# Graph layer 1 with own terms computed two blocks ahead, batch norm's mean from column sums, and variances summed by VectorE

## The chip, the cores and the metric

The kernel runs on one core of one Trainium2 chip. The metric is the device time of one execution in microseconds (us). Of the kernel before there are three runs; their median is 1605.33 us (1604.46 to 1609.47).

A core has five engines with a queue each: TensorE (PE, matmuls; PEld is its weight load), VectorE (DVE), ScalarE (ACT), GpSimd (POOL) and SyncE (SP). Each works through its queue in order. An instruction that waits for a semaphore holds up all that stand behind it on the same queue. SP issues the plain DMAs, POOL the indirect ones (gathers and scatters by a list of row numbers).

## The reference

Four graph layers over 2,708 nodes of 128 features and a sparse 2708 x 2708 adjacency matrix (about 16 entries in a row and the diagonal). Each is added to its input and normalised:

```python
x = _layernorm(x + _L0_gnn_ref(x, adj))   # (adj.T @ x) / column sums of adj
x = _layernorm(x + _L1_gnn_ref(x, adj, ...))
x = _layernorm(x + _L2_gnn_ref(x, adj, ...))
x = _layernorm(x + _L3_gnn_ref(x, adj, ...))   # attention, four heads
```

The two layers that matter here:

```python
# layer 1
s = x @ msg_w[:, :D].T
d = x @ msg_w[:, D:].T
messages = gelu(s[:, None, :] + d[None, :, :] + msg_b)
aggregated = einsum('ijd,ij->id', messages, adj)
new = concatenate([x, aggregated], -1) @ upd_w.T + upd_b
h = gelu(new) + x
out = (h - mean(h)) / sqrt(var(h) + eps) * ln_w + ln_b
# layer 2
h = A @ (x @ W) + b
mean = h.mean(axis=0)
var = ((h - mean) ** 2).mean(axis=0)
h = gamma * (h - mean) * rsqrt(var + eps) + beta
out = where(h >= 0, h, 0.2 * h)
```

## The kernel before

The nodes stand in 22 blocks of 128 (the last has 20). While layer 0's sums run, the kernel searches each adjacency row for its entries and makes lists of them (DVE: `extract`), ranks the nodes by their number of entries and sorts them, so that a block needs only as many message slots as its longest list (`CAPS`, 368 slots in all). Layer 0 ends with `layer0`, which writes each node's terms `d` to the table `d_dram`, and its pair of `d` and normalised `x` to `dx_dram`, scattered by rank (L781).

The loop of layer 1 (L974) takes the blocks one turn after another in the order `TURNS`. A turn has these parts:

- `own_row` (L818) loads the block's sorted rows `x_s` from `dx_dram`, one turn ahead.
- `messages` (L827) takes the one bank of the PSUM pool `own_ps` as tile `own`. PE transposes `x_s` into it (L832), ACT copies it out (`x_st`, L833), PE multiplies it with the weights and adds the bias (L834, L835): the own terms, which stay in the same bank. Then the block's message slots come in chunks of up to eight: POOL gathers one row for each node and slot from `d_dram` (L856), DVE adds the own terms to a chunk (L858), ACT applies the gelu (L861), and DVE multiplies each slot with the adjacency value and sums it, in two running sums in the same bank (`weigh`, L846). The last of each goes to `parts` in SBUF. The chunks rotate through five buffers (`msgs`, L812).
- `spread` (L594), called at the end of `messages`, prepares lists for layer 3. DVE multiplies (L601), PE multiplies into the bank `own` (L607), DVE copies out twice (L614, L615), for two groups in most turns.
- In the first turns, `transposed` (L906) and `extract` go through the nine blocks that layer 0 left over. `transposed` writes the adjacency matrix's transpose to `at_dram` in pieces that rotate through three buffers `at_sb`; later turns do that for the other thirteen blocks.
- `update` (L868) takes the one bank of the pool `tail_ps` as tile `tail`: PE sums and transposes `parts` (L872), ACT copies (L879), PE makes the new features (L881 to L883), ACT applies the gelu (L888), DVE adds `x_s` (L889). Then two layer norms follow. Each takes its variance by `deviation` (L294): ACT squares and sums (L301), DVE makes the root by some eight small steps (`rsqrt`). The result `x_n` (L319) is scattered to `x2_dram` by POOL (L898), transposed by PE (L899) and multiplied with layer 2's weights (L903, L904).
- From turn 11 on `layer2` (L950) gathers two blocks of rows of `at_dram` per turn, and PE adds them to layer 2's sums in six banks (L957).

The order on each queue is made by a scheduler from the order of the calls, except in the part before layer 1, where DVE's order is written by hand. So the scatter of L898 stands on POOL's queue between gathers of later blocks.

The batch norm after layer 2 first adds the bias to all 22 blocks (L1052) while PE sums their columns with a matrix of ones (L1054); it makes the mean from this (L1065), subtracts it (L1069), squares on ACT (L1070) and sums the squares with PE again (L1072). Layer 3 follows, with 400 gathers of its own.

Of the kernel before, what the change touches and what calls it, by code (L numbers as in the profile page):

```python
# [81 lines left out]
GOT = 9  # L82


@with_exitstack
def gnn_resnorm_kernel(
# [126 lines left out]
    dx_dram = tables.tile([NBLK * P, 2 * D], FP, name="dx_dram")  # L213
# [80 lines left out]
    def deviation(small, n, count, h, sums, newton=True):  # L294
# [5 lines left out]
        for j in range(count):  # L300
            nc.scalar.activation(  # L301
                junk[0:n], h[:, j, :], AF.Square, bias=sums[:, j : j + 1],
                accum_out=var[0:n, j : j + 1],
            )
# [10 lines left out]
    def normalised(small, n, count, h, sums, dst, newton=True):  # L315

        var = deviation(small, n, count, h, sums, newton)
        for j in range(count):
            nc.vector.tensor_scalar(  # L319
                dst[:, j, :], h[:, j, :], sums[:, j : j + 1], var[0:n, j : j + 1],  # L320
                ALU.add, ALU.mult,
            )
# [12 lines left out]
    with ExitStack() as layer:  # L335
# [6 lines left out]
        sums_ps = part.enter_context(tc.tile_pool(name="sums_ps", bufs=7, space=PSUM))  # L342
        hand.enter_context(tc.manual_schedule(engines={engine.DVE}))
# [26 lines left out]
        def weight(src, name):  # L370
            raw = small.tile([P, P], FP, name="raw_w")
# [107 lines left out]
        def ranking(g):  # L479
# [17 lines left out]
            key_row = work.tile([P, SPLIT, P], FP, name="key_row")  # L497
# [213 lines left out]
        nc.vector.tensor_copy(deg[0:NREM, NFULL : NFULL + 1], tails[0:NREM, 3:4])  # L711
        nc.vector.tensor_scalar(zero, deg, 0.0, None, ALU.is_equal)
# [6 lines left out]
        def layer0(b0, count, n):  # L719
# [32 lines left out]
            dx = brief.tile([P, count, 2, D], FP, name=f"dx{count}", bufs=3 if count > 1 else 2)  # L752
            for j in range(count):
                nc.vector.tensor_scalar(
                    dx[0:n, j, 1, :], h[0:n, j, :], sums[:, j : j + 1], v[:, j : j + 1],
# [5 lines left out]
            for j in range(count):  # L761
                nc.tensor.transpose(
                    pt[:, j * P : j * P + n], dx[0:n, j, 1, :], ident[0:n, 0:n]
# [4 lines left out]
            for j in range(count):  # L768
# [4 lines left out]
            nc.scalar.copy(dx[0:n, :, 0, :], pm[0:n, 0:count])  # L773
            nc.sync.dma_start(
                d_dram[b0 * P : b0 * P + w, :].rearrange("(b p) w -> p b w", p=n),
                dx[0:n, :, 0, :],
# [3 lines left out]
            for j in range(count):  # L780
                did = scatter(  # L781
                    dx_dram, rank[0:n, b0 + j : b0 + j + 1],
                    dx[0:n, j].rearrange("p t d -> p (t d)"),
# [28 lines left out]
        msgs = layer.enter_context(tc.tile_pool(name="msgs", bufs=5))  # L812
# [5 lines left out]
        def own_row(b):  # L818
            n = BLOCKS[b][1]
            x_s = mine.tile([P, 2, D], FP, name="x_s", bufs=3)  # L820
            nc.sync.dma_start(
                x_s[0:n],
                dx_dram[b * P : b * P + n, :].rearrange("p (t d) -> p t d", t=2),
# [3 lines left out]
        def messages(b, x_s, three):  # L827
            n, kk = BLOCKS[b][1], CAPS[b]
            po = own_ps.tile([P, 512], FP, name="own", tag="own")
            x_st, s_ps = mine.tile([P, P], FP, name="x_st"), po[:, P : 2 * P]  # L830
            acc = (po[:, 0:P], po[:, 3 * P : 4 * P])
            nc.tensor.transpose(po[:, 0:n], x_s[0:n, 1, :], ident[0:n, 0:n])  # L832
            nc.scalar.copy(x_st[:, 0:n], po[:, 0:n])  # L833
            nc.tensor.matmul(s_ps[0:n], lhsT=x_st[:, 0:n], rhs=ws_t, start=True, stop=False)  # L834
            nc.tensor.matmul(  # L835
                s_ps[0:n], lhsT=ones[0:1, 0:n], rhs=msgb[0:1, :], start=False, stop=True
            )
# [11 lines left out]
            nc.vector.tensor_tensor(mk, mk, s_ps[0:n], ALU.add)  # L849
            nc.scalar.activation(mk, mk, AF.Gelu)  # L850
            weigh(0, mk)
            for c0, c1 in chunks_of(kk):
                kc = c1 - c0
                msg = msgs.tile([P, 8, D], FP, name="msg")
                for k in range(kc):
# [3 lines left out]
                    mk, mk, s_ps[0:n].unsqueeze(1).to_broadcast((n, kc, D)), ALU.add  # L859
# [4 lines left out]
            for i, b3 in enumerate(three):  # L864
                spread(b3, po, 256 + 64 * i)
            return x_st, parts

        def update(b, x_s, x_st, parts):  # L868
# [16 lines left out]
            x_n = mine.tile([P, 1, D], FP, name="x_n")  # L885
# [6 lines left out]
            rstd = deviation(mine, n, 1, new[0:n], s0)  # L892
# [4 lines left out]
            normalised(mine, n, 1, new[0:n], s1, x_n[0:n])  # L897
            scatter(x2_dram, perm[0:n, b : b + 1], x_n[0:n, 0, :])  # L898
# [5 lines left out]
            nc.scalar.copy(xw[0:n, b, :], px)  # L904

        def transposed(b, rows, cleared=False):  # L906
# [10 lines left out]
            for j0 in range(0, NBLK, 4):  # L917
                count = min(4, NBLK - j0)
                pt = bank.tile([P, 4, P], FP, name="pt_a", tag="bank")
                at = small.tile([P, 4, P], FP, name="at_sb", bufs=3)  # L920
# [28 lines left out]

        def layer2(k):  # L950
# [3 lines left out]
            gather(at[0:n, :], at_dram, perm[0:n, b : b + 1])  # L954
            for ib in range(NBLK) if k == 0 else ORDER:
                i0, m = BLOCKS[ib]
                nc.tensor.matmul(  # L957
# [14 lines left out]
        ahead = own_row(0)  # L972
        left = list(range(SPLIT, NBLK))
        for i, b in enumerate(TURNS):  # L974
            if i == SPLIT - 2:
                sorted_lists(1)
            x_s, ahead = ahead, own_row(TURNS[i + 1]) if i + 1 < NBLK else None
# [6 lines left out]
            x_st, agg = messages(b, x_s, three)  # L984
            for _ in range(2 if i < 1 else 1):
                if left:
# [5 lines left out]
                    if e == NBLK - 1:  # L992
                        run(place(NBLK - 2, NBLK, lists(NBLK - 2, NBLK)))
            update(b, x_s, x_st, agg)
# [7 lines left out]
            if i >= 11:  # L1002
                for k in range(2 * (i - 11), min(i, 2 * (i - 10))):
                    layer2(k)
        layer2(NBLK - 1)
# [24 lines left out]
    with ExitStack() as layer:  # L1030
# [17 lines left out]
        ps_m = own_ps.tile([P, 512], FP, name="ps_m", tag="own")  # L1048
        ps_v = tail_ps.tile([P, 512], FP, name="ps_v", tag="tail")
        for b0, count, n in quads():  # L1050
            a = accs2[b0 // 4].rearrange("p (j d) -> p j d", d=D)[0:n, b0 % 4 : b0 % 4 + count]
            nc.vector.tensor_tensor(hb[0:n, b0 : b0 + count], a, broad(b_row, n, count), ALU.add)  # L1052
            for b in range(b0, b0 + count):
                nc.tensor.matmul(  # L1054
                    ps_m[:, 0:D], lhsT=ones[0:n, :], rhs=hb[0:n, b, :],
                    start=(b == 0), stop=(b == NBLK - 1),
# [6 lines left out]
        mean = work.tile([P, D], FP, name="bn_mean")  # L1063
# [968 lines left out]
```

## Time and profile before

| | us |
|---|---|
| median of three runs | 1605.33 |
| the profiled execution | 1957.99 |
| its span, first to last instruction | 1956.3 |
| layer 0, search and lists | 0 to about 229 |
| layer 1 and layer 2's sums | 229 to 1053 |
| batch norm and tables of layer 3 | 1053 to 1165 |
| layer 3 | 1165 to 1956 |

The profiled execution is 22% longer than the median, so a time read from it is larger than its share of an unprofiled run. In the whole span PE is busy 1248.6 us (64%), DVE 1173.2 (60%), ACT 768.6 (39%), POOL 896.4 (46%). In a line of the profile's timeline stand the start, the duration, the engine, the line of the kernel, the operation, what it writes and reads, and in brackets the idle time of the engine before it with what ended it. In a line of waits stand the waiting operation, what it waited for, the sum in us, how often, and the longest. "issue" is time in which the profile shows no wait, though a wait for several semaphores can be booked to the wrong one. POOL's busy time for an indirect DMA is that of its issue.

### The profile page before, as it was taken

To read this page: it belongs to the slowest core of one execution; us is meant where nothing else is said; L and a number is where in the kernel's file an instruction comes from. 1 tells how busy PE (TensorE), PEld (TensorE's weight loads), DVE (VectorE), ACT (ScalarE), POOL (GpSimd) and SP (SyncE) were. 2 spreads that over 40 slices of the span, in tenths; PEclk is the share of its full clock that TensorE was granted. 3 is DMA by queue.
4 is the path that set the end of the run, shared out by engine and by line. 5 is a ranking of instruction groups with operands and counts; after the bars stand their busy time and mean duration, and the time that the engine had idled before them with its cause. 6 is when DMAs were issued, how large, how long until landed. Compare 5 with 4: busy or idle time off the path is not lost. (4 is left out here: it accounts for less than half of the span.)

```text
span 1956.3 us, 23628 instructions
## 1 busy us (share of the span) xinstructions
PE 1248.6 (64%) x5771; PEld 866.9 (44%) x5771; DVE 1173.2 (60%) x4900; ACT 768.6 (39%) x3134; POOL 896.4 (46%) x996
## 2 busy tenths in 40 slices
PE   7972414443345564556585647888798888877884
PEld 7972313333234453445465313445444444444444
DVE  8999536763353533343346626677678777676773
ACT  3475424542222311111111414455455555455543
POOL 1002655555544445444430454555565556555430
PEclk9985655555555576666677755677677777677675
DMA  8541547765444624332331474766475665756530
GB/s 288 228 160 41 170 94 195 202 169 145 125 90 117 173 96 96 109 132 88 141 110 37 153 222 130 190 189 194 140 206 178 173 178 153 189 159 191 153 109 7
DMA packets 164926, 289.61 MB, mean 148 GB/s; under 512 B 46850, under 2 KB 118752, under 8 KB 157679
## 3 DMA queue, kind: packets, MB, share of 16 engines
q0 software_dynamic: 60496, 190.76, 34.4%
q1 hardware_dynamic: 96739, 92.56, 15.6%
q10 hardware_dynamic: 7544, 4.69, 0.9%
q8 instruction: 48, 0.79, 0.2%
q14 instruction: 99, 0.81, 0.1%
HBM read 242.50 MB, written 45.35 MB: 147 GB/s over the span
## 5 line engine op out<-in xcount | busy, mean ns | idle before, releaser
L245 POOL DMA_INDIRECT g<-t_dram,idx x400 | 402.2, 1005 | 310.8 <-issue 169.2
L245 POOL DMA_INDIRECT msg<-d_dram,idx x368 | 348.7, 947 | 272.1 <-issue 225.7
L1324 ACT ACTIVATE sum_junk<-g 126x128 bf16<-126x128 f32 (+3 forms) x1024 | 302.6, 298 | 142.3 <-issue 60.8
L1293 PE MATMUL z<-x,copies 32*126 32x512 f32 (+3 forms) x800 | 220.3, 917 | 60.7 <-DVE g L1490 33.9
L957 PE MATMUL acc<-x_nat,at_rows 128*128 128x128 f32 (+2 forms) x968 | 168.8, 335 | 64.5 <-issue 52.6
L931 PE MATMUL pt_a<-ident,rows 128*128 128x128 f32 (+2 forms) x475 | 119.0, 408 | 131.5 <-ACT at_sb L936 106.9
L1490 DVE TENSOR_TENSOR g<-g,z 126x1536 f32<-126x1536 f32 (+3 forms) x100 | 175.1, 1751 | 40.1 <-remote 25.4
L1324 ACT ACTIVATION_READ_ACCUMULATOR sum_junk<-g 126x1 f32 (+3 forms) x1024 | 193.5, 189 | 0.0
L957 PEld LDWEIGHTS acc<-x_nat,at_rows 128*128 128x128 f32 (+2 forms) x968 | 151.2, 240 | 78.8 <-issue 67.5
L1298 PE MATMUL z<-g,ident 126*126 126x512 f32 (+3 forms) x200 | 168.5, 937 | 0.1
L1370 PE MATMUL po_s<-wm,g 126*128 126x24 f32 (+6 forms) x800 | 124.7, 310 | 59.7 <-DVE wm L1357 53.8
L931 PEld LDWEIGHTS pt_a<-ident,rows 128*128 128x128 f32 (+2 forms) x475 | 86.4, 212 | 154.8 <-ACT at_sb L936 120.9
L1370 PEld LDWEIGHTS po_s<-wm,g 126*128 126x128 f32 (+3 forms) x800 | 120.8, 237 | 75.1 <-DVE wm L1357 63.8
L1316 DVE SCALAR_TENSOR_TENSOR g<-g,a_ps 126x1536 f32<-126x1536 f32 (+6 forms) x100 | 151.1, 1511 | 0.0
L406 PE MATMUL acc<-x_nat,rows 128*128 128x129 f32 (+3 forms) x1012 | 128.5, 288 | 25.9 <-DMA rows<-in_adj_dram 15.1
L406 PEld LDWEIGHTS acc<-x_nat,rows 128*128 128x128 f32 (+2 forms) x1012 | 122.9, 197 | 31.1 <-DMA rows<-in_adj_dram 16.1
L846 DVE SCALAR_TENSOR_TENSOR own<-msg,ls,own 128x128 f32<-128x128 f32 (+1 forms) x302 | 106.5, 353 | 37.4 <-remote 13.5
L1293 PEld LDWEIGHTS z<-x,copies 32*126 32x126 f32 (+3 forms) x800 | 65.3, 250 | 97.9 <-issue 54.2
L1308 DVE SCALAR_TENSOR_TENSOR g<-z,a 126x128 f32<-126x128 f32 (+3 forms) x400 | 92.0, 287 | 19.4 <-DMA g<-t_dram,idx 9.4
L431 DVE FIND_INDEX8 ci<-cv,rows 128x8 uint32<-128x247 f32 (+2 forms) x242 | 101.6, 420 | 0.0
L436 DVE MAX8 cv<-rows 128x8 f32<-128x247 f32 (+2 forms) x242 | 98.0, 411 | 2.2 <-POOL rows L396 2.2
L1298 PEld LDWEIGHTS z<-g,ident 126*126 126x126 f32 (+3 forms) x200 | 41.7, 261 | 122.1 <-issue 109.1
(293 smaller groups left out, 2084.0 us busy)
## 6 DMA issues: line engine op xcount, KB each, us to landing
rows<-in_adj_dram SPq DMA_DIRECT2D x34, 1354.0 KB
at_dram<-at_sb SPq DMA_DIRECT2D x105, 256.0 KB
g<-t_dram,idx POOLq DMA_INDIRECT x400
msg<-d_dram,idx POOLq DMA_INDIRECT x368
t_dram<-t_row SPq DMA_DIRECT2D x21, 256.0 KB
x_s<-dx_dram SPq DMA_DIRECT2D x21, 128.0 KB
at_dram<-at_sb SPq DMA_DIRECT2D x21, 64.0 KB
d_dram<-dx SPq DMA_DIRECT2D x5, 256.0 KB
```

Of the source, the lines that this page charges most:

```text
L245: nc.gpsimd.indirect_dma_start(out=dst, out_offset=None, in_=table[0:N, :], in_offset=bass.IndirectOffsetOnAxis(ap=index, axis=0),)
L406: nc.tensor.matmul(accs0[k][0:m, c0 : c0 + f1 - f0], lhsT=rows[0:n, j0 : j0 + m], rhs=x_nat[0:n, b, f0:f1], start=k not in started, stop=( ...
L431: nc.vector.max_index(out=ci[0:n, at], in_max=cv[0:n, at], in_values=rows[0:n, c0 : c0 + cw])
L846: nc.vector.scalar_tensor_tensor(to, m, v, last, ALU.mult, ALU.add)
L931: nc.tensor.transpose(pt[0:m, j, 0:n], rows[0:n, c0 : c0 + m], ident[0:n, 0:n])
L957: nc.tensor.matmul(accs2[ib // 4][0:m, (ib % 4) * D : (ib % 4 + 1) * D], lhsT=at[0:n, i0 : i0 + m], rhs=xw[0:n, b, :], start=(k == 0 and i ...
L1293: nc.tensor.matmul(z3[0:e, r, :] if r < 3 else z1[0:e], lhsT=copies[g][rows, j, :], rhs=own[b][1][rows, :], start=True, stop=r < 3, skip_g ...
L1298: nc.tensor.matmul(z1[0:e], lhsT=ident[0:e, 0:e], rhs=g4[0:e, 3, 0:HD], start=False, stop=True, skip_group_check=True,)
L1316: nc.vector.scalar_tensor_tensor(z, z, 0.0, a_ps[0:e].unsqueeze(1).to_broadcast((e, count, HD)), ALU.max, ALU.mult)
L1324: nc.scalar.activation(junk[0:e], g4[0:e, r, hd * D : (hd + 1) * D], AF.Identity, accum_out=sc[0:e, r, hd : hd + 1],)
L1370: nc.tensor.matmul(po[:, p0 * HEADS : (p0 + g) * HEADS], lhsT=g4s[i][0:e, r, HD : HD + D], rhs=wm[0:e, 4 * i + r, :, :], start=True, stop= ...
L1490: nc.vector.tensor_tensor(z, z, z3[0:e], ALU.add)
```

## The change

- Own terms: a new function `own_terms` computes `x_st` and the own terms for a block two turns ahead, in the bank of `tail_ps` (shared with `update`), and copies them to SBUF as `s`. `messages` reads `s`. The bank of `own_ps` is taken once, as `sums1`, and held for all turns: it keeps the running sums and, in columns that alternate from turn to turn, the spread steps. Row loads go out three turns ahead (`x_s` has four buffers).
- The scatter of a block's rows is no longer called in `update` but in `put_results`, after the `messages` of the next turn.
- `msgs` has six buffers, `at_sb` five. Two tiles of the first part move to a pool `head` that is given back before layer 1.
- The variances of `update` are made by DVE: it subtracts the mean into `centred` and squares and sums that.
- Batch norm's mean: layer 0's column sums of the adjacency matrix (`column_sums`) go as one more column into the scattered rows of `dx_dram` and are loaded in sorted order by one DMA of single elements. In `layer2` ACT spreads a block's column over a tile `weighed`, and PE multiplies it with the same right side into a free part of the sixth bank of sums, so that the columns' sum over all nodes is there with the last block. The first pass of the batch norm and its matmuls with ones go away; the bias and the mean are one row, `shift`.

```diff
-    dx_dram = tables.tile([NBLK * P, 2 * D], FP, name="dx_dram")
+    DX = 2 * D + 1
+    dx_dram = tables.tile([NBLK * P, DX], FP, name="dx_dram")
...
         for j in range(count):
+            if here:
+                centred = small.tile([P, D], FP, name="centred", bufs=1)
+                nc.vector.tensor_scalar(
+                    centred[0:n], h[:, j, :], sums[:, j : j + 1], None, ALU.add
+                )
+                nc.vector.scalar_tensor_tensor(
+                    junk[0:n], centred[0:n], 1.0, centred[0:n], ALU.mult, ALU.mult,
+                    accum_out=var[0:n, j : j + 1],
+                )
+                continue
...
+        column_sums = work.tile([P, 24], FP, name="column_sums")
+        nc.vector.tensor_copy(column_sums, deg)
...
-            nc.scalar.copy(dx[0:n, :, 0, :], pm[0:n, 0:count])
+            nc.scalar.copy(dx[0:n, :, 0:D], pm[0:n, 0:count])
+            nc.gpsimd.tensor_copy(
+                dx[0:n, :, 2 * D : DX], column_sums[0:n, b0 : b0 + count].unsqueeze(2)
+            )
...
-        msgs = layer.enter_context(tc.tile_pool(name="msgs", bufs=5))
+        msgs = layer.enter_context(tc.tile_pool(name="msgs", bufs=MSGS))
...
-        def messages(b, x_s, three):
+        def own_terms(b, x_s):
+
+            n = BLOCKS[b][1]
+            tp = tail_ps.tile([P, 512], FP, name="terms", tag="tail")
+            x_st = mine.tile([P, P], FP, name="x_st", bufs=3)
+            s = mine.tile([P, D], FP, name="s", bufs=3)
+            nc.tensor.transpose(tp[:, 0:n], x_s[0:n, 1, :], ident[0:n, 0:n])
+            nc.scalar.copy(x_st[:, 0:n], tp[:, 0:n])
+            pn = tp[0:n, P : 2 * P]
+            nc.tensor.matmul(pn, lhsT=x_st[:, 0:n], rhs=ws_t, start=True, stop=False)
+            nc.tensor.matmul(pn, lhsT=ones[0:1, 0:n], rhs=msgb[0:1, :], start=False, stop=True)
+            nc.scalar.copy(s[0:n], pn)
+            return x_s, x_st, s
+
+        def messages(b, x_s, s, three, spreads):
             n, kk = BLOCKS[b][1], CAPS[b]
-            po = own_ps.tile([P, 512], FP, name="own", tag="own")
-            x_st, s_ps = mine.tile([P, P], FP, name="x_st"), po[:, P : 2 * P]
-            acc = (po[:, 0:P], po[:, 3 * P : 4 * P])
-            nc.tensor.transpose(po[:, 0:n], x_s[0:n, 1, :], ident[0:n, 0:n])
-            nc.scalar.copy(x_st[:, 0:n], po[:, 0:n])
-            nc.tensor.matmul(s_ps[0:n], lhsT=x_st[:, 0:n], rhs=ws_t, start=True, stop=False)
-            nc.tensor.matmul(
-                s_ps[0:n], lhsT=ones[0:1, 0:n], rhs=msgb[0:1, :], start=False, stop=True
-            )
+            acc = (sums1[:, 0:P], sums1[:, 3 * P : 4 * P])
...
-                    mk, mk, s_ps[0:n].unsqueeze(1).to_broadcast((n, kc, D)), ALU.add
+                    mk, mk, s[0:n].unsqueeze(1).to_broadcast((n, kc, D)), ALU.add
...
-                spread(b3, po, 256 + 64 * i)
-            return x_st, parts
+                spread(b3, sums1, P + 128 * (spreads % 2) + 64 * i)
+            return parts
...
-            normalised(mine, n, 1, new[0:n], s1, x_n[0:n])
-            scatter(x2_dram, perm[0:n, b : b + 1], x_n[0:n, 0, :])
+            normalised(mine, n, 1, new[0:n], s1, x_n[0:n], here=True)
+            results.append((b, x_n))
...
+        def put_results():
+            while results:
+                b, x_n = results.pop(0)
+                n = BLOCKS[b][1]
+                scatter(x2_dram, perm[0:n, b : b + 1], x_n[0:n, 0, :])
...
-                at = small.tile([P, 4, P], FP, name="at_sb", bufs=3)
+                at = small.tile([P, 4, P], FP, name="at_sb", bufs=5)
...
+        column_sum = keep.tile([P, NBLK], FP, name="column_sum")
+        for b0, b1, n in ((0, NFULL, P), (NFULL, NBLK, NREM)):
+            nc.sync.dma_start(
+                column_sum[0:n, b0:b1],
+                dx_dram[b0 * P : b0 * P + (b1 - b0 - 1) * P + n, 2 * D : DX].rearrange(
+                    "(b p) o -> p (b o)", p=n
+                ),
+            )
...
+            weighed = small.tile([P, P], FP, name="weighed", bufs=1)
+            nc.scalar.activation(
+                weighed[0:n], ones[0:n], AF.Copy, scale=column_sum[0:n, b : b + 1]
+            )
             for ib in range(NBLK) if k == 0 else ORDER:
                 i0, m = BLOCKS[ib]
+                if ib == 21:
+
+                    nc.tensor.matmul(
+                        accs2[5][:, 2 * D : 3 * D], lhsT=weighed[0:n], rhs=xw[0:n, b, :],
+                        start=False, stop=False,
+                    )
...
-        ahead = own_row(0)
+        sums1 = own_ps.tile([P, 512], FP, name="sums1", tag="own")
+        rows1 = [own_row(b) for b in TURNS[:3]]
+        terms = [own_terms(b, rows1.pop(0)) for b in TURNS[:2]]
...
-            x_s, ahead = ahead, own_row(TURNS[i + 1]) if i + 1 < NBLK else None
+            x_s, x_st, s = terms.pop(0)
+            if i + 3 < NBLK:
+                rows1.append(own_row(TURNS[i + 3]))
...
-            x_st, agg = messages(b, x_s, three)
+            agg = messages(b, x_s, s, three, i)
+            put_results()
...
+            if rows1:
+                terms.append(own_terms(TURNS[i + 2], rows1.pop(0)))
             update(b, x_s, x_st, agg)
...
-        ps_m = own_ps.tile([P, 512], FP, name="ps_m", tag="own")
         ps_v = tail_ps.tile([P, 512], FP, name="ps_v", tag="tail")
+        nc.vector.scalar_tensor_tensor(
+            mean, accs2[5][:, 2 * D : 3 * D], 1.0 / N, b_row, ALU.mult, ALU.add
+        )
+        nc.vector.tensor_tensor(shift, b_row, mean, ALU.subtract)
         for b0, count, n in quads():
             a = accs2[b0 // 4].rearrange("p (j d) -> p j d", d=D)[0:n, b0 % 4 : b0 % 4 + count]
-            nc.vector.tensor_tensor(hb[0:n, b0 : b0 + count], a, broad(b_row, n, count), ALU.add)
-            for b in range(b0, b0 + count):
+            h = hb[0:n, b0 : b0 + count]
+            sq = small.tile([P, 4, D], FP, name="bn_sq")
+            nc.vector.tensor_tensor(h, a, broad(shift, n, count), ALU.add)
+            nc.scalar.activation(sq[0:n, 0:count], h, AF.Square)
+            for j in range(count):
                 nc.tensor.matmul(
-                    ps_m[:, 0:D], lhsT=ones[0:n, :], rhs=hb[0:n, b, :],
-                    start=(b == 0), stop=(b == NBLK - 1),
+                    ps_v[:, 0:D], lhsT=ones[0:n, :], rhs=sq[0:n, j, :],
+                    start=(b0 + j == 0), stop=(b0 + j == NBLK - 1),
                 )
```

## The prediction

> **What bounds the kernel now.** I read the busy shares by stage first, then GpSimd's waits in layer 1, then its order in time, then one turn of the node loop, then the batch norm. Layer 1 and the sums of layer 2 run from 229 to 1053 us of a span of 1956.3 us. No engine is full there (columns: stretch, length, then busy us and instructions of PE, weight loads, DVE, ACT, POOL; clock, DMA share, GB/s):
>
> ```profile
> 229.00:698.00 469.00, 198.81 (x811) 155.50 (x812) 230.22 (x1099) 165.87 (x341) 232.57 (x245) 0.54 0.57 151
> 698.00:987.00 289.00, 158.87 (x879) 137.18 (x879) 106.65 (x436) 37.86 (x100) 146.76 (x155) 0.68 0.32 102
> ```
>
> So waits bound it. The queue with the longest steady work is POOL: an indirect DMA starts every 1.25 us (0.95 busy, 0.30 between, from the timeline below), so the 155 of the late stretch need 194 us of its 289, and the 245 of the early one 306 of 469. POOL's waits from 698 to 987 us:
>
> ```profile
> POOL msg L245 <- issue: 56.1, 133, 15.9
> POOL x_dram L253 <- DVE own L846: 49.8, 5, 14.1
> POOL x_dram L253 <- DVE x_n L319: 35.1, 3, 17.2
> ```
>
> The scatter of a finished block's rows waits for them, and every gather behind it on the queue waits too. In time, one such place:
>
> ```profile
> 740.69 0.95 POOL L245 DMA_INDIRECT at_rows<-at_dram,perm  x1 [0.31 <-issue]
> 741.94 0.95 POOL L245 DMA_INDIRECT at_rows<-at_dram,perm  x1 [0.30 <-issue]
> 756.55 1.00 POOL L253 DMA_INDIRECT x_dram<-x_n,perm  x1 [13.67 <-DVE own L846]
> ```
>
> Why the rows are late shows in the turn after 853 us. The last sums of the messages end at 853.66; the next block's transpose needs the same PSUM bank `own` and starts at 865.80, after both spread steps went through it one after the other; its first message add starts at 872.53:
>
> ```profile
> 853.05 0.61 DVE L846 SCALAR_TENSOR_TENSOR parts<-msg,ls,own 128x128 f32<-128x128 f32 x2
> ...
> 865.58 0.17 DVE L615 CAST idx<-own 125x20 int32<-125x20 f32 x1
> ...
> 865.80 0.48 PE L832 MATMUL own<-ident,x_s 128*128 128x128 f32 x1 [3.02 <-issue]
> ...
> 870.59 0.26 ACT L833 COPY x_st<-own 128x128 f32<-128x128 f32 x1
> ...
> 872.53 0.29 DVE L849 TENSOR_TENSOR x_s<-x_s,own 128x128 f32<-128x128 f32 x1 [1.31 <-PE own L835]
> ```
>
> That is 18.9 us in which no message of the next block is used; the messages themselves then take from 872.5 to 886.6, 14 us. The batch norm starts with two passes in series:
>
> ```profile
> 1053.24 0.69 DVE L1052 TENSOR_TENSOR hb<-acc,b_row 128x512 f32<-128x512 f32 x1 [9.00 <-PE acc L957]
> ...
> 1059.80 3.48 DVE L1069 TENSOR_TENSOR hb<-hb,bn_mean 128x512 f32<-128x512 f32 x7
> ```
>
> **What the Trainium skill says.** Its page "Perfetto Trace Analysis", section "DMA Instruction — SWDGE (GPSIMD)", says that the profiled interval of a DMA from GpSimd ends when the descriptors are written. The trace agrees: a gather of 128 rows of 512 bytes takes 947 ns and one of 128 rows of 10,832 bytes 946 ns. So POOL's pace counts instructions, not bytes. The same page, "Optimization Strategy", says that bubbles that repeat can mean that no buffer is free for the next tile; the bank above is such a case. Its section "Optimizing Scalar/DVE Operations" makes a VectorE operand in PSUM dearer than one in SBUF (about 125 against 60 ns). Here the add with a PSUM operand (L849) takes 289 ns and that with SBUF alone (L877) 284, so I book nothing for `s` in SBUF. "SBUF — State Buffer", section "SBUF: two separate sides", says that a VectorE operation with two SBUF inputs, or in a two-port mode, can hold a port that GpSimd needs; no row here isolates it. It gives a rival below.
>
> **The change part by part** (sums in the profiled execution's time).
>
> Bank held, own terms two blocks ahead, scatter moved. The transpose, the copy, two matmuls and their waits leave the head of the turn, and the spread steps no longer stand between two blocks. The built order confirms it: on DVE the spread multiplies now stand between message sums or small steps, and on POOL the scatter of block b stands 7 to 11 message chunks behind the block's last gather (turns 0 to 15) against 4 to 7 before. The waits that can go are 289 - 194 = 95 us from 698 to 987 us, and one of 5.4 at 1004.7. The last two scatter waits (10.1 and 16.6 us) come after the last gather and stay. Not all of the 95 is free. A turn still costs DVE its 13 us (106.65 over the eight turns) with dependent steps between, and PE the update. With turns of 36 us now (scatters 11 to 19 of 22 lie at 697.7 and 987.1, 289.4 us for eight turns) and POOL at 24, I take two thirds: 63 us, bounds 20 and 95. With the 5: 68.
>
> Early stretch, 229 to 698. POOL waits 163 us, mostly for message buffers. DVE also searches nine adjacency blocks here (242 MAX8 and 242 FIND_INDEX8 over 22 blocks, 98.0 and 101.6 us: 9 us a block) and is busy 230 us. A sixth buffer and the freed bank help less where DVE holds the work: 15 us, bounds -10 and 60.
>
> Variance on VectorE. Two ScalarE passes of 0.40 + 0.19 us leave per block; a subtract (0.35, as L319) and a square with sum (0.29 + 0.08, as L889) come twice. That is 1.4 us more DVE per block, 32 us in all, beside gathers while POOL sets the pace; uncovered it costs up to 32. Only the last block's chain is bare: about 1 us gained. Already inside the "two thirds".
>
> Batch norm. The pass to 1059.80 goes (6.56 us); two small operations come (0.29 each): 6 us gained, bare, since all later stages wait. `weighed` (22 ScalarE passes of about 0.4, as L916) and 22 matmuls of two 0.28 passes, 12 us of PE, lie in stretches where PE is busy 55%: nothing, at most 12.
>
> Column sums. Seven copies on POOL stand among the scatters of `dx_dram`, which run back to back from 215.8: some 0.3 us each, 2 us lost (bounds 0 and 4; the nearest rows are POOL's small iotas and memsets, 0.11 to 0.3). Their load moves 2,708 elements of 4 bytes. The like of it exists, the load of `diag`, and its issue held ScalarE's queue for 13.32 us:
>
> ```profile
> 16.27 13.32 ACTq L669 DMA_DIRECT2D diag<-in_adj_dram  x1
> ```
>
> It now stands on SP ahead of the first three row loads, and the first `weighed` waits for it on ScalarE ahead of the first `x_st` copy, with the gelus behind. The first add comes some 13 us later; POOL, with six chunks of buffers (45 gathers, 56 us), goes on. I take 5 us lost, bounds 0 and 13.
>
> Five `at_sb` buffers instead of three: ScalarE waits 16.1 us in all for these stores; off the path, nothing. Rows of 1,028 bytes, `head` and the fourth `x_s`: nothing. Row loads go out two turns earlier on SP.
>
> Sum: 68 + 15 + 1 + 6 - 2 - 5 = 83 us of 1957.99 (span 1956.3). That execution is 22% longer than the median of 1605.33; I scale by 1605.33 / 1957.99 = 0.82 and get 68: 1537 us.
>
> **The rivals.** (1) The waits move from the scatter to the message buffers, since DVE's and PE's turn, not the bank, sets the pace. For it: in the early stretch POOL waits for buffers already. Against it: DVE is busy only 107 of 289 us. Then a fifth of the 95, 19, stays, with 6 - 7 = -1 from the rest, 18 x 0.82 = 15: 1590 us.
> (2) Slower: own terms and update now share the single bank `tail`. The update held it from 857.7 (L872) to 883.6 (L904), 26 us; the own terms held `own` for 6.7 (865.80 to 872.5). In series 33 us: under the turn of 36, so it doesn't decide, unless a turn of both grows past 36, say by PE's order, since terms of b+2 stand ahead of the sums of b. Each us above costs 22. At 2.5 above, 55 x 0.82 = 45: 1650 us.
> (3) The port: 55 adds of about 1.0 us and 44 subtracts of 0.35 hold GpSimd off, up to 70 us, which cancels most of 83: 1595 to 1603 us, no change at worst. Against it: gathers keep 895 to 1077 ns through everything that DVE does now.
>
> **How the numbers follow.** Forecast 0.60 (1537; its own range 1500 to 1570), rival 1 0.22, rival 2 0.11, rival 3 0.07. Changes under 0.3% (5 us) can't be told from none. Faster: 0.60 + 0.22 + 0.02 of rival 3 = 0.84; same 0.05; slower 0.11. The low end is all of the 95 and half of the early bound: (95 + 5 + 30) x 0.82 = 107, 1498, and a little more: 1492. The high end takes in rival 1: 1598.
>
> **What would show it.** POOL's scatter waits before the last gather fall from 90 to under 20 us, its waits on messages don't rise by as much, and 987 moves to about 900 us. The first batch norm add and the first square lie 1 us apart. SP shows one issue of about 13 us near 230. Wrong: large POOL waits on `msg` in the late stretch (rival 1), PE waiting on `tail` or `terms` for longer each turn (2), or gathers over 1.1 us (3).

## The result: 1.0% slower

| | us | ratio to the kernel before |
|---|---|---|
| kernel before, median of 13 runs | 1606.28 | |
| kernel after, median of 13 runs | 1622.20 (1610.94 to 1631.08) | 1.0096, 95% interval 1.0073 to 1.0118 |
| forecast | 1537 (1492 to 1598) | |

The forecast had the sign wrong. Its profile is the first thing to look at again. The kernel before takes one of two times, about 1605 us in some series of runs and about 1950 us in others (medians 1934 and 1957, on other chips than the first; why is not known), and the profile that the prediction read, 1957.99 us, is of the second kind. A second profile of the kernel before, called *base* below, has a span of 1606.3 us, and the profile of the kernel after one of 1629.4, from the longest of its 13 runs. These two are compared; their difference of 23 us is more than the 16 between the medians.

First the stretch from the first to the last message gather of layer 1, by engine (stretch, length, then busy us and instructions of PE, weight loads, DVE, ACT, POOL; clock, DMA share, GB/s). The kernel before in the prediction's profile:

```profile
229.00:1014.00 785.00, 379.15 (x1806) 310.29 (x1807) 347.95 (x1583) 208.78 (x455) 396.02 (x417) 0.60 0.47 131
```

The kernel before in base:

```profile
231.00:793.00 562.00, 319.16 (x1781) 268.07 (x1782) 335.75 (x1538) 204.80 (x447) 396.37 (x417) 0.67 0.62 180
```

The kernel after:

```profile
231.00:806.00 575.00, 324.37 (x1737) 273.89 (x1736) 326.86 (x1639) 196.95 (x400) 412.92 (x416) 0.66 0.61 177
```

POOL does the same 417 instructions in the same 396 us in both profiles of the kernel before; only its waits differ. With 0.31 us between two indirect DMAs as the normal gap, the waits beyond it sum to 261 us in the prediction's profile (157 at message gathers, 101 at the scatters of L253) and to 38 in base (13 and 22). So at 1605 us POOL is close to its own pace through the whole layer, and there were 38 us to win there, not 163 + 95. In the kernel after POOL is busy 16.6 us longer with one instruction less.

The waits of POOL in that stretch in base (who waited for whom, sum, times, longest):

```profile
POOL msg L245 <- issue: 113.9, 312, 7.2
POOL x_dram L253 <- DVE x_n L319: 17.0, 1, 17.0
```

and in the kernel after:

```profile
POOL msg L249 <- issue: 97.7, 319, 0.6
POOL x_dram L257 <- DVE x_n L333: 12.0, 2, 6.4
POOL lists_dram L257 <- DVE rs_t L271: 11.2, 1, 11.2
POOL lists_dram L257 <- DMA lists_dram<-lists,rank: 5.5, 1, 5.5
```

Under "issue" the longest wait before a message gather fell from 7.2 to 0.6 us: what is left there is the 0.3 us gap, 319 times. What was gained there (11 us) and at the scatter (9 us) came back at the scatter of the lists (17 us more). The costliest group of POOL in layer 1, from the page of base (busy us, mean ns, idle before):

```profile
L245 POOL DMA_INDIRECT msg<-d_dram,idx x368 | 349.1, 949 | 132.2 <-issue 113.9
```

and of the kernel after:

```profile
L249 POOL DMA_INDIRECT msg<-d_dram,idx x368 | 365.2, 992 | 118.4 <-issue 97.7
```

The same 368 gathers take 16.1 us longer. The timeline of the kernel after shows one of them:

```profile
620.01 0.94 POOL L249 DMA_INDIRECT msg<-d_dram,idx  x1 [0.30 <-issue]
621.20 1.22 DVE L884 TENSOR_TENSOR msg<-msg,s 128x1024 f32<-128x1024 f32 x1 [9.83 <-issue]
621.25 1.99 POOL L249 DMA_INDIRECT msg<-d_dram,idx  x1 [0.30 <-issue]
623.55 0.94 POOL L249 DMA_INDIRECT msg<-d_dram,idx  x1 [0.30 <-issue]
```

The message add runs from 621.20 to 622.42; the gather that starts just after it ends at 623.24, 0.82 us after the add. The same meeting in base, where the own terms lie in PSUM, leaves the gather alone:

```profile
245.27 1.09 DVE L858 TENSOR_TENSOR msg<-msg,own 128x896 f32<-128x896 f32 x1 [3.37 <-DMA msg<-d_dram,idx]
245.36 0.94 POOL L245 DMA_INDIRECT msg<-d_dram,idx  x1 [0.30 <-issue]
```

Worked out over the whole timeline: of the 37 indirect DMAs of the kernel after that had a message add running 0.12 us after their own start, 33 end 0.78 to 0.86 us after the end of that add; in base 3 of 43 do, by chance, and their lengthening sums to nothing. An add that begins when a gather is well under way doesn't lengthen that one.

The trace shows a second thing, at the PSUM bank `tail`, which the update of a block and the own terms of a later one now share. Seven instructions around one update (parts are the finished sums of a block's messages):

```profile
712.63 0.34 DVE L872 SCALAR_TENSOR_TENSOR parts<-msg,ls,sums 128x128 f32<-128x128 f32 x1
...
722.05 0.71 PE L898 MATMUL tail<-ident,parts 128*128 128x128 f32 x4 [0.35 <-ACT s L858]
...
744.40 0.27 ACT L930 COPY x_nat<-tail 128x128 f32<-128x128 f32 x1 [0.58 <-PE tail L929]
...
744.72 0.33 PE L853 MATMUL terms<-ident,x_s 128*128 128x128 f32 x1
...
746.34 0.27 ACT L858 COPY s<-terms 128x128 f32<-128x128 f32 x1 [0.35 <-PE terms L857]
...
746.64 0.29 DVE L875 TENSOR_TENSOR x_s<-x_s,s 128x128 f32<-128x128 f32 x1 [3.56 <-ACT s L858]
...
746.88 0.61 PE L898 MATMUL tail<-ident,parts 128*128 128x128 f32 x4
```

The sums of a block are ready at 712.97, but its update starts at 746.88: first comes the update of the block before (722.05 to 744.67), then the own terms of a later block (744.72 to 746.61). On average a block's sums wait 26.1 us for their update, in base 2.6. An update holds the bank for 22.3 us and own terms for 2.9, and from the first update at 304 us to the last at 849 the bank is held 98.5% of the time, without a gap over 1 us; in base, by updates alone, 88%. Nor are the own terms early: in 15 of the 22 blocks the first add that reads `s` starts within 0.1 us of the end of its copy. VectorE's first use of the own terms in base and in the kernel after (busy us, mean ns, idle before):

```profile
L849 DVE TENSOR_TENSOR x_s<-x_s,own 128x128 f32<-128x128 f32 x21 | 6.0, 287 | 21.4 <-PE own L835 21.3
L875 DVE TENSOR_TENSOR x_s<-x_s,s 128x128 f32<-128x128 f32 x21 | 6.1, 290 | 48.2 <-ACT s L858 48.2
```

The batch norm starts 22 us later than in base, though the last message gather starts only 13 us later. The last block's sums are even just 3 us late (815.9 against 813.1), but its update starts 20 us after them, in base 2. So two things can have cost time, longer gathers and the shared bank, and the experiments have to tell them apart.

### The profile page after: what moved, and what is told of

It is laid out like the page before. It is cut to its first block, busy times and chain, and to the rows that moved or that the text cites. A ratio compares the mean times of both kernels' runs of the same rounds, so it can differ in the third digit from the quotient of the medians.

```text
span 1629.4 us, 23721 instructions
## 1 busy us (share of the span) xinstructions
PE 1175.2 (72%) x5771; PEld 828.0 (51%) x5771; DVE 1159.0 (71%) x5027; ACT 757.8 (47%) x3090; POOL 910.2 (56%) x1003
## 5 line engine op out<-in xcount | busy, mean ns | idle before, releaser
L249 POOL DMA_INDIRECT msg<-d_dram,idx x368 | 365.2, 992 | 118.4 <-issue 97.7
L1351 PE MATMUL z<-x,copies 32*126 32x512 f32 (+3 forms) x800 | 208.5, 865 | 26.6 <-DVE g L1548 25.2
L1010 PE MATMUL acc<-x_nat,at_rows 128*128 128x128 f32 (+2 forms) x968 | 156.6, 324 | 49.1 <-DMA at_rows<-at_dram,perm 48.8
L965 PE MATMUL pt_a<-ident,rows 128*128 128x128 f32 (+2 forms) x475 | 100.7, 375 | 114.7 <-ACT at_sb L970 103.8
L1010 PEld LDWEIGHTS acc<-x_nat,at_rows 128*128 128x128 f32 (+2 forms) x968 | 141.6, 230 | 59.9 <-DMA at_rows<-at_dram,perm 45.1
L1356 PE MATMUL z<-g,ident 126*126 126x512 f32 (+3 forms) x200 | 162.5, 906 | 6.0 <-DMA g<-t_dram,idx 6.0
L421 PEld LDWEIGHTS acc<-x_nat,rows 128*128 128x128 f32 (+2 forms) x1012 | 123.6, 198 | 28.4 <-DMA rows<-in_adj_dram 13.3
L1428 PE MATMUL po_s<-wm,g 126*128 126x24 f32 (+6 forms) x800 | 116.1, 297 | 30.3 <-DVE wm L1415 28.4
L1428 PEld LDWEIGHTS po_s<-wm,g 126*128 126x128 f32 (+3 forms) x800 | 112.6, 223 | 47.3 <-DVE wm L1415 41.1
L884 DVE TENSOR_TENSOR msg<-msg,s 128x896 f32<-128x896 f32 (+4 forms) x55 | 57.6, 1049 | 80.4 <-DMA msg<-d_dram,idx 64.0
L872 DVE SCALAR_TENSOR_TENSOR sums<-msg,ls,sums 128x128 f32<-128x128 f32 (+1 forms) x302 | 105.6, 350 | 2.2 <-ACT msg L887 1.7
```

The source lines that it names most:

```text
L249: nc.gpsimd.indirect_dma_start(out=dst, out_offset=None, in_=table[0:N, :], in_offset=bass.IndirectOffsetOnAxis(ap=index, axis=0),)
L421: nc.tensor.matmul(accs0[k][0:m, c0 : c0 + f1 - f0], lhsT=rows[0:n, j0 : j0 + m], rhs=x_nat[0:n, b, f0:f1], start=k not in started, stop=( ...
L872: nc.vector.scalar_tensor_tensor(to, m, v, last, ALU.mult, ALU.add)
L965: nc.tensor.transpose(pt[0:m, j, 0:n], rows[0:n, c0 : c0 + m], ident[0:n, 0:n])
L1010: nc.tensor.matmul(accs2[ib // 4][0:m, (ib % 4) * D : (ib % 4 + 1) * D], lhsT=at[0:n, i0 : i0 + m], rhs=xw[0:n, b, :], start=(k == 0 and i ...
L1351: nc.tensor.matmul(z3[0:e, r, :] if r < 3 else z1[0:e], lhsT=copies[g][rows, j, :], rhs=own[b][1][rows, :], start=True, stop=r < 3, skip_g ...
```

## The experiments

Theory: the message adds with both inputs in SBUF hold off the gathers, on the queue that paces layer 1. Rivals: another part (the shared bank `tail`, batch norm and column sums, variances on VectorE, scatter) costs the time. Ratios are to the kernel before, in the same series of runs; 0.1% is 1.6 us, and times of different series are compared by these ratios.

**base.** The kernel before, unchanged.

> The kernel before, profiled once more. The prediction's sum rests on 95 us of GpSimd waits between 698 and 987 us of an execution that lasted 1957.99 us. Theory 1 (those waits belonged to that one execution, and in an ordinary one GpSimd issues its indirect DMAs of layer 1 nearly without a pause): span near 1605 us, layer 1 some 610 to 640 us long instead of 824, and under 20 us of waits for x_n or parts at the scatter before the last gather. Theory 2 (the waits are real and the change put others in their place): some 50 to 95 us of scatter waits here too.

1607.97 us, span 1606.3. Layer 1's message stretch is 562 us long instead of 785. Of the scatter waits 21.6 us are there, slightly above the bound of theory 1, and 17.0 of them are one wait. The 95 us are not there.

**before_s.** One thing of the change in the kernel before:

```diff
+            s = mine.tile([P, D], FP, name="s")
+            nc.scalar.copy(s[0:n], s_ps[0:n])
-            nc.vector.tensor_tensor(mk, mk, s_ps[0:n], ALU.add)
+            nc.vector.tensor_tensor(mk, mk, s[0:n], ALU.add)
-                    mk, mk, s_ps[0:n].unsqueeze(1).to_broadcast((n, kc, D)), ALU.add
+                    mk, mk, s[0:n].unsqueeze(1).to_broadcast((n, kc, D)), ALU.add
```

> The kernel before with one thing of the change: ScalarE copies the own terms to SBUF and the message adds read them there, so that both inputs of an add lie in SBUF. Port theory (such an add keeps GpSimd from its port): gathers that start beside an add last up to 2 us, their mean goes from 947 to about 990 ns, and the kernel is 12 to 25 us slower (1618 to 1630 us). Rival (where the operand lies costs nothing; the loss comes from another part): within 5 us of before, since one ScalarE copy of 0.3 us in a turn is all that is added, and gathers stay at 947 ns.

Ratio 1.0060 (1.0035 to 1.0085), 10 us: just under the expected band, outside the rival's. The gathers did what was expected; the group in its trace (busy us, mean ns, idle before):

```profile
L245 POOL DMA_INDIRECT msg<-d_dram,idx x368 | 360.3, 979 | 127.1 <-issue 101.8 <-DMA msg<-d_dram,idx 5.5 <-ACT at_sb L938 4.6
```

11.2 us longer than in base, and 33 of the 44 that meet an add end 0.78 to 0.86 us after it. This is the one run in which the place of the operand changes alone, but for one more ScalarE copy in each block.

**own_psum.** The kernel after with the own terms in PSUM.

```diff
-            s = mine.tile([P, D], FP, name="s", bufs=3)
...
-            pn = tp[0:n, P : 2 * P]
-            nc.tensor.matmul(pn, lhsT=x_st[:, 0:n], rhs=ws_t, start=True, stop=False)
-            nc.tensor.matmul(pn, lhsT=ones[0:1, 0:n], rhs=msgb[0:1, :], start=False, stop=True)
-            nc.scalar.copy(s[0:n], pn)
...
+            s = sums1[:, 2 * P : 3 * P]
+            nc.tensor.matmul(s[0:n], lhsT=x_st[:, 0:n], rhs=ws_t, start=True, stop=False)
+            nc.tensor.matmul(s[0:n], lhsT=ones[0:1, 0:n], rhs=msgb[0:1, :], start=False, stop=True)
...
-                spread(b3, sums1, P + 128 * (spreads % 2) + 64 * i)
+                spread(b3, sums1, P + 64 * i)
```

> The kernel after, but the own terms are made in the held bank at the head of the turn and the message adds read them from PSUM again (the transpose and x_st stay two blocks ahead; the spread steps no longer alternate columns). Port theory: gathers back to a mean of 947 ns, 15 to 20 us less than after: 1600 to 1607 us, so ratio to before 0.995 to 1.001. Rival (the shared tail bank, the column sums or the order of the queues is what costs): the time stays at 1615 to 1630 us.

1594.37 us, ratio 0.9926 (0.9898 to 0.9954): a larger gain than expected, and faster than both kernels. Its gathers (same columns):

```profile
L249 POOL DMA_INDIRECT msg<-d_dram,idx x368 | 348.7, 948 | 121.7 <-issue 101.1 <-DMA msg<-d_dram,idx 6.1 <-ACT at_sb L968 3.1
```

The message stretch is 33 us shorter than in the kernel after: 18 us less busy time of POOL and 15 us fewer waits, mostly at the scatter of the lists. But the edit changes two things. It also takes two matmuls and the copy of the own terms out of the bank `tail`: own terms hold it for 0.8 us instead of 2.9, the bank is held 91% of the time instead of 98.5%, and a block's sums wait 3.7 us for their update instead of 26.1. So the rival of the shared bank isn't excluded, and what each of the two is worth here stays open.

**split_adds.** The kernel after with one add for each slot:

```diff
-                nc.vector.tensor_tensor(
-                    mk, mk, s[0:n].unsqueeze(1).to_broadcast((n, kc, D)), ALU.add
-                )
+                for k in range(kc):
+                    nc.vector.tensor_tensor(msg[0:n, k, :], msg[0:n, k, :], s[0:n], ALU.add)
```

> The kernel after, but each message slot gets its own add (368 adds of 128x128 in place of 55 of up to 128x1024), both inputs in SBUF as before. It costs VectorE about 50 us more (368 x 0.28 = 103 against 55). In the kernel after, gathers last 20.8 us longer in sum than 0.95 us each. Theory A (GpSimd is held off until the one running instruction ends, so the length of the instruction counts): that excess falls below 6 us. Theory B (it is the share of time with two SBUF inputs that counts): it doubles to 35 us or more. The time itself is 1610 to 1650 us under both, since VectorE has more work.

The excess fell from 20.8 to 7.6 us, with 43 us more of such adds (368 with 100.2 us in sum, against 57.6). That is near theory A's 6 and far from B's 35; the rest may come from adds that follow one another closely. Ratio 1.0043 (1.0029 to 1.0057): 8 us better than the kernel after in spite of the added work. So the length of one instruction counts. The bank `tail` is still held 97% of the time, and the kernel is still slower than before.

**var_act** and **psum_var_act.** The variances by ScalarE again, once in the kernel after, once in own_psum:

```diff
-            rstd = deviation(mine, n, 1, new[0:n], s0, here=True)
+            rstd = deviation(mine, n, 1, new[0:n], s0)
...
-            normalised(mine, n, 1, new[0:n], s1, x_n[0:n], here=True)
+            normalised(mine, n, 1, new[0:n], s1, x_n[0:n])
```

> The kernel after, with the variances of layer 1 squared and summed by ScalarE again. Port theory in its narrow form (the long message adds do the harm, 18 us): the 88 short operations here, about 0.3 us each with the squares alone having two SBUF inputs, matter 0 to 5 us: 1615 to 1622 us. Rival (the extra work on VectorE, some 30 us in all, is the loss): 1600 to 1608 us.

> own_psum (1594.37 us) with the variances of layer 1 squared and summed by ScalarE again. Theory 1 (the square stands on ScalarE's queue behind gelus that wait for gathers, so the scatter comes late and holds up GpSimd, as between after and var_act, where the scatter waits rose from 13 to 48 us): 10 to 25 us slower than own_psum, 1605 to 1620 us. Rival (that loss needs the longer gathers too, and with the adds in PSUM GpSimd has the slack): within 5 us of own_psum.

Both missed, in opposite directions: var_act 1.0259 (1.0223 to 1.0295), psum_var_act 0.9839 (0.9815 to 0.9863), the fastest kernel of the study at 1580.72 us. With slow gathers the squares on ScalarE cost 26 us beside the kernel after; with fast ones they gain 14 beside own_psum. The waits of POOL in var_act show where the loss lies:

```profile
POOL x_dram L257 <- DVE x_n L333: 22.1, 3, 14.3
POOL x_dram L257 <- DVE sums L872: 20.7, 5, 5.1
```

In all 48 us at the scatter against 13 in the kernel after. Each square stands in ScalarE's queue among gelus that wait, over VectorE's adds, for gathers. I argue that this makes the rows, and so the scatter, late, and the scatter then holds the next gathers; it isn't shown by a run of its own. Of psum_var_act's gain, 18 us lie before the batch norm (its first instruction at 816.2 us, in base at 834.0) and 11 after it, 10 of them behind the first scaling, where the code is the same; that part is not explained.

**bn_only.** The batch norm and column sum part of the diff alone, in the kernel before.

> The kernel before with the batch norm part alone (column sums in the scattered rows, seven copies on GpSimd, the load of single elements, 22 products with the sums of layer 2, one pass less in the batch norm). By the prediction's steps: 6 us gained in the batch norm, 2 lost by the copies, 5 lost by the load: 1 us gained, 1600 to 1608 us. Rival A (copies and load are hidden, as the traces suggest: the first message gather starts at 231.9 us in the kernel after and at 231.6 before): 6 us gained, 1597 to 1601 us. Rival B (the weighed products or the load in SP's queue are the hidden loss of the change): slower than before by 3 us or more.

Ratio 1.0067 (1.0047 to 1.0087): 11 us slower, rival B's side. In its trace the first gather starts 2.0 us later than in base (233.6 against 231.6), as the prediction booked for the seven copies; by gather 144 the lag is 11.9 us, 7 of it from the scatter of the lists on, and there it stays. The first weighed product comes only after that. So the products didn't cause this lag, and what did isn't settled.

**after_nobn** and **psum_var_nobn.** The same part taken out of the kernel after and out of psum_var_act.

> The kernel after with the batch norm of the kernel before: adds of two SBUF inputs, held bank, late scatter, variances on VectorE. If bn_only's 11 us hold here too: 1609 to 1614 us. If the batch norm part gains its 6 us here: 1625 to 1630 us.

> psum_var_act (1580.72 us) with the batch norm of the kernel before again. What is left of the change is what the prediction's first step spoke of: the held bank, x_st two blocks ahead, the late scatter and the buffers; message adds read PSUM and ScalarE makes the variances, as before. If the batch norm part costs what bn_only showed (0.67%, 11 us): 1567 to 1573 us. If it costs only where the turns are long, and gains its 6 us here: 1583 to 1588 us. The prediction's first two steps gave 68 us for it (1537); the waits of the second profile of before allow at most 38 (1567).

after_nobn 1.0082 (1.0050 to 1.0114), no difference from the kernel after; psum_var_nobn 0.9900 (0.9861 to 0.9938), 1586.06 us: here the part gains some 10 us by the ratios, 5 by the medians, and the intervals touch. Minus 11, 0 and plus 5 to 10 us in three surroundings: it has no price of its own. psum_var_nobn is also the nearest to the prediction's first two steps without the SBUF adds: it has the held bank, the transposes two blocks ahead, the late scatter and the buffers, though the own terms themselves are made at the head of the turn. It gains 1.0%, not 4%.

**psum_var_w4.** One number changed in psum_var_act: `weighed` with `bufs=4` for `bufs=1`.

> psum_var_act (1580.72 us) with four buffers for the tile weighed in place of one. In its trace ScalarE waits 56 us for the one buffer to come free of TensorE's previous product (75 us between 540 and 860 us in the kernel after), with the gelus of the messages behind it in its queue. If these waits are on the path: 1565 to 1577 us, and the batch norm part is no longer a loss. If they are covered, as ScalarE is busy under half of the time: within 4 us of psum_var_act.

0.9909 (0.9878 to 0.9940): slower than psum_var_act, which neither expectation had. The wait of ScalarE for that buffer fell from 56.1 to 22.4 us. It is longest in the kernel after:

```profile
ACT weighed L999 <- PE acc L1006: 74.9, 17, 15.8
```

The sum looks like a loss, and taking most of it away in psum_var_act didn't help: a long wait in a table is not by itself on the path. Why it made things worse stays open.

**put_only.** The late scatter alone, in the kernel before (with three buffers for `x_n`, as in the kernel after):

```diff
-            scatter(x2_dram, perm[0:n, b : b + 1], x_n[0:n, 0, :])
+            results.append((b, x_n))
...
             x_st, agg = messages(b, x_s, three)
+            put_results()
```

> The kernel before with one thing of the change: the scatter of a block's rows is issued after the messages of the next turn. In the second profile of the kernel before, GpSimd waits 21.6 us at these scatters between its first and its last message gather. Theory 1 (GpSimd's queue sets the pace there): 5 to 20 us of them are recovered, 1585 to 1600 us. Rival (the wait moves to the message buffers or to the next scatter): within 5 us of before.

1.0012 (0.9991 to 1.0033): nothing. POOL's waits at the scatter are 20.6 us, in base 21.6.

**psum_var_put.** psum_var_act with the scatter in `update`.

> psum_var_act (1580.72 us) with the scatter of a block's rows called in update again, as in the kernel before. The prediction put most of its gain on the waits at this scatter. put_only showed no gain from the late call alone. If the late call pays once the own terms are ahead: 1586 to 1600 us. If the held bank and the early terms do the work and the place of the scatter doesn't matter: within 4 us of psum_var_act.

1928.75 us, with 1956.60 for the kernel before: ratio 0.9851 (0.9811 to 0.9890). It can't be set against psum_var_act's 1580.72 us. Three more kernels ran beside a kernel before of 1934.16 us:

> The kernel after once more, in the same job as the next two. The prediction was summed from an execution of 1957.99 us; the last job shows that this is no accident of one execution, since the kernel before took 1956.6 us in all of its 11 runs there. If this job runs at that pace: the prediction's own terms would give 83 us less than before (ratio 0.958); with longer gathers alone and waits that hide part of them, ratio 0.99 to 1.01. If it runs at the ordinary pace: 1.007 to 1.012 as in the first comparison.

> The fastest kernel so far once more, beside after and the next one on the same chip: ratio to before 0.981 to 0.987 at either pace.

> psum_var_act with the scatter called in update, as in the kernel before; its first run took place where all kernels took 22% longer (ratio 0.985 there), so it could not be set against psum_var_act. If the late call pays: 0.4 to 1% slower than psum_var_act in this job. If the place of the scatter doesn't matter: within 0.3%.

after_again 1.0036 (1.0007 to 1.0066), psum_var_act_again 0.9904 (0.9882 to 0.9926), psum_var_put_again 0.9930 (0.9903 to 0.9957). So the change doesn't gain in executions like the one that the prediction read, either. The last two overlap, so the place of the scatter isn't shown to matter. POOL's waits in after_again:

```profile
POOL x_dram L257 <- DVE x_n L333: 83.4, 7, 27.3
POOL msg L249 <- ACT at_sb L970: 55.0, 6, 20.8
POOL x_dram L257 <- DMA at_dram<-at_sb: 24.0, 1, 24.0
POOL x_dram L257 <- DVE spread L616: 22.4, 3, 10.5
```

With the bank `own` taken once for all turns, the scatters wait 131 us beyond the normal gap, more than the 101 of before. But `tail` is held 99% of the time, and a block's sums wait 39.7 us for their update, against 3.2 in the prediction's profile. In psum_var_act_again they wait 5.1, and 86 us of scatter waits remain.

## Why the prediction was wrong, by its own steps

**The step that failed** is the first: "The waits that can go are 289 - 194 = 95 us", with two thirds, 63 us, taken. It failed in two ways. The waits were read from an execution of 1957.99 us and brought to 1605 us by one factor, 0.82. But POOL's busy time is 396 us in both, and only its waits are shorter: 261 us became 38. And the relief did not come. The step says that the own terms and their waits "leave the head of the turn"; in the kernel after they queue for `tail`, and VectorE waits 48.2 us for them instead of 21.3. Where the large scatter waits do exist, after_again has more of them, 131 us, and psum_var_act_again, where the updates start in time, still 86 of 101. The scatter waits for `x_n`, the end of a chain through TensorE, ScalarE and VectorE; that the bank `own` set its end is not borne out, and what does is not settled.

**`s` in SBUF: booked at nothing, and it cost 8 to 10 us.** The argument compared the add's own duration (289 against 284 ns), which is right: a 128x896 add takes 1084 ns with PSUM and 1091 without. The cost appears on another engine: before_s, with little else changed, is 10 us slower than before, and split_adds wins 8 back. Between the kernel after and own_psum it is 1.7% or 27 us, of which 18 are POOL's busy time, but there the bank is relieved as well. So a loss by the operand is shown, and that it alone decided the sign is not. Rival 3 named the mechanism and set it aside at 0.07 because "gathers keep 895 to 1077 ns through everything that DVE does now". That was no evidence: before, every message add had one input in PSUM, so none of the kind in question had run beside a gather. The Trainium skill, page "SBUF — State Buffer", section "SBUF: two separate sides", says that a VectorE operation with two SBUF inputs and a GpSimd operation that reads SBUF exclude each other for a whole instruction. The trace agrees in one direction: the gather ends 0.82 us after the add, while the adds are no longer than in base (at most 1.23 and 1.22 us). That it is the reading of the row numbers (`idx`, in SBUF) which waits is not shown.

**Early stretch, 15 us.** Over the whole stretch of messages their waits did fall, from 13 to 2 us. The lists' scatter took 17 back.

**Variances, 1 us.** The gain from VectorE's variances depends on the rest: 26 us beside the SBUF adds, a loss of 14 us with the own terms in PSUM. Counting busy time could not give it.

**Batch norm, 6 us.** The predicted sign is in the timeline of the kernel after, the first square 0.72 us after the first add:

```profile
857.25 3.46 DVE L1122 TENSOR_TENSOR hb<-acc,bn_shift 128x512 f32<-128x512 f32 x7
857.97 1.23 ACT L1123 ACTIVATE bn_sq<-hb 128x512 f32<-128x512 f32 x2 [8.90 <-DVE hb L1122]
860.64 1.27 DVE L1131 TENSOR_TENSOR w_prod<-w_s,a_all 128x512 f32<-128x512 f32 x2
874.73 0.69 DVE L1178 TENSOR_TENSOR hb<-hb,bn_scale 128x512 f32<-128x512 f32 x1
```

and in base:

```profile
834.00 0.69 DVE L1052 TENSOR_TENSOR hb<-acc,b_row 128x512 f32<-128x512 f32 x1 [9.10 <-PE acc L957]
837.46 1.27 DVE L1060 TENSOR_TENSOR w_prod<-w_s,a_all 128x512 f32<-128x512 f32 x2
853.21 0.67 DVE L1120 TENSOR_TENSOR hb<-hb,bn_scale 128x512 f32<-128x512 f32 x1
```

From the batch norm's first instruction (`bn_mean` at 856.45 us, the first add at 834.00) to the first scaling it takes 18.3 and 19.2 us: 0.9 gained, not 6. The pass that went had covered VectorE's work for layer 3's tables, `w_prod` among it, which now stands beside the squares and behind them. It was not bare.

**Column sums.** The copies cost the 2 us that were booked (bn_only). The load was priced by `diag`; its two issues take 1.77 us, not 13.3 (start, duration):

```profile
230.85 1.77 SPq L986 DMA_DIRECT2D column_sum<-dx_dram  x2
```

**Rivals 1 and 2.** Rival 1 doesn't decide: no large message waits in the late stretch. Rival 2, own terms and update in series on one bank, was set aside because 33 us fit under a turn of 36. Both figures came from the long execution. In base a turn takes 24.8 us, and the update holds `tail` for 21.7 of them, so with 2.9 us of own terms no slack is left; the trace of the kernel after shows the queue that this rival feared. What it costs is open: the turns are not longer (24.2 us), but the first update starts 20.6 us later than in base and this is never made up, and no run takes the own terms out of `tail` and nothing else.

## What to carry to other kernels

Before summing terms, set the profiled execution against the median: if they differ clearly (here by 22%), take another profile, since waits don't scale with the total. When an operand moves between PSUM and SBUF, ask which other engine meets that operation, not only what the operation itself costs; beside a GpSimd queue of gathers, a long VectorE operation with two SBUF inputs is paid for by the gathers, and one input in PSUM or shorter operations avoid most of it. When work moves to a bank that another step uses, add up how long each holds it within one turn. A saved pass is a gain only if nothing else ran under it.

## What the runs showed of the hardware

- A gather of 128 rows lasts 0.94 us alone. If an add with two SBUF inputs is running 0.12 us after its start, it ends 0.82 us after the add (33 of 37 cases, up to 1.99 us in all). With one input in PSUM there is no effect (own_psum: 0.1 us in sum over 44 meetings).
- Small edits shift the time by some 10 us either way (the batch norm part costs 11 us in bn_only and gains 5 to 10 in psum_var_act; one buffer count, in psum_var_w4, costs 11), and the traces don't settle why. A sum of parts is no better than that here.
